# A hand-written order for VectorE and ScalarE in a fused time-mix and feed-forward kernel

## The chip, the cores and the metric

The kernel runs on one core of a Trainium2 chip. A core has engines with a queue of instructions each: TensorE (PE, matrix products; PEld are its weight loads), VectorE (DVE), ScalarE (ACT), GpSimd (POOL), and SyncE (SP), whose queue issues nearly all DMA transfers of this kernel. They meet through semaphores. The metric is the time of one execution on the device, in microseconds, smaller being better. The median of three runs of the kernel before is 883.06 us, the lowest 882.07 and the highest 883.17.

## What is computed

The input `x` holds 4 sequences of 1024 tokens with 512 features. Each token is normalised (`xn`), and two branches are added to `x`. The reference, cut to what matters:

```python
xn = _layernorm(x)
# branch 1: time mixing, HIDDEN = 704
xx = concatenate([xn[:, 1:2], xn[:, :-1]], axis=1) - xn
k = (xn + xx * time_mix_k) @ Wk.T
r = (xn + xx * time_mix_r) @ Wr.T
w = exp(-exp(time_decay))
state_t = state_{t-1} * w + relu(k_t)          # a scan over the tokens
out = (state * r) @ Wv.T
att = (out - mean) * rsqrt(var + EPS) * ln_gamma + ln_beta
# branch 2: feed-forward, 2048 hidden features
D = gelu(float16(xn) @ W0.T + bias0).astype(float16)
ffn = (D @ W1.T + bias1).astype(float16)
return x + att + ffn
```

So each token's mixed input is a blend of its own normalised vector and that of the token before it: `xn + (prior - xn) * m`, which is the same as `xn * (1 - m) + prior * m`.

## The kernel before

The 4096 tokens are worked on in 8 blocks of 512 (two blocks to a sequence); `i` is the block in work, `j = i + 1` the next one, prepared while `i` runs. Inside a block a loop over `n` from 0 to 15 walks through the 16 chunks of 128 hidden features of the feed-forward branch. One iteration puts on TensorE, in this order:

- `up` (L738): the product into the bank `pd` for the chunk two iterations ahead, 8 matmuls. ScalarE then makes gelu of it and a cast (`d`).
- `down` (L766): the products of chunk `n` into the four banks `pe`, which add up over the whole block, 8 matmuls.
- a "piece" of the time-mixing branch. In blocks 1 to 7, n=0 to 4 are the `k` pieces and n=7 to 11 the `r` pieces (`three_pass`, L586: 8 matmuls into `pa`, 4 into `pb`); n=5 and 6 are the two half pieces (`half_pass`, L614: 8 matmuls into `ph`); n=12 to 15 are the output pieces, one for each 128 tokens. In blocks 0 and 1 the output pieces use unsplit operands (`po`), and tokens are dealt with in pairs; from block 2 on they are three-pass products (`out_three_pass`, L682: `oa` and `ob`). In the last block two output pieces share n=12 and two share n=13, and the last four chunks of `down` are left to the end.

The banks `pd`, `pa`, `pb`, `ph`, `oa`, `ob` and `po` come from one pool of four; `pe` from another pool of four.

A piece returns a function, its "follower", that is called one iteration later, behind the next `up`. It empties the banks: `a` on ScalarE (L604), `y` from `pb` and `a` on VectorE (L605); then, for a `k` piece, relu on ScalarE (L607) and the scan on VectorE (L491) into a state tile; for an `r` piece the product with the state (L508) and the split of the result; for an output piece the layer norm's statistics (L303, L304), the reciprocal root on POOL (L297, L298) and three operations on VectorE that end in adding to the residual (L672, L677, L678).

Operands are split into exact parts so that fewer passes of the matrix engine give full precision: `split_x` (L281) makes a truncated value `u` (VectorE, L235), its copy `h` (ScalarE, L284), the rest `l` (VectorE, L285) and a combined term `m` (VectorE, L286).

Besides pieces there is background work, put at chosen iterations: the split of the mixed `r` input (`split_xr`), the next block's load of `x`, its statistics, its normalisation, its 16 transposes (L329), its float16 copies (`x16`), and at the end of a block its mixing (`mixed`, L344, one of four pieces of 128 features at a time). The mixing takes `xx` as the difference of the prior token and the token (L354) and blends twice (L357), all on VectorE, then splits the `k` input. At the head of iteration 14 four ScalarE copies (`ffn_input`) make the next block's `xf`. In block 1 there is more: the `wr` weights are split (`split_kr`) and stored to memory, `wv` is split (`split_wv`), and the low parts of W0 are stored (`store_w0l`). After n=15 four operations on VectorE (`rounded`, L723) take the four sums out of `pe`; in the next block's n=0 and 1, `finish` (L728) adds them to the residual and SP stores the result.

What sets the order: inside `tc.manual_schedule(engines=...)` the named engines issue what the block holds in the order in which it is written; an engine that is not named is ordered by the framework's scheduler. Block 0 and what comes before it name TensorE, VectorE, ScalarE and SyncE. From block 1 on only TensorE and SyncE are named (L831), so VectorE and ScalarE are ordered by the scheduler; POOL is always ordered by it. The end of the kernel (L965) names TensorE and VectorE.

Tiles come from pools with a fixed number of places: 63 `part` tiles (tag `q`) hold the split operands, the states and the weights that stay; 5 `temp` tiles (tag `s`) hold short-lived values; `x` has one place for both the next block's input and the residual. Whoever writes a new tile waits until a place is free.

Of the kernel before, what the change touches and what calls it, by code (L numbers as in the profile page):

```python
# [22 lines left out]
def time_mix_and_gelu_ffn(  # L23
# [30 lines left out]
    nc = tc.nc  # L54
# [226 lines left out]
    def split_x(raw, name):  # L281
        u = truncated(raw, f"u{name}")
        h, l, m = (part(f"{p}{name}") for p in "hlm")
        nc.scalar.copy(h, u)  # L284
        nc.vector.tensor_sub(l, raw, u)  # L285
        nc.vector.scalar_tensor_tensor(m, l.bitcast(F32), -S, u, ALU.mult, ALU.add)  # L286
        return h, l, m
# [55 lines left out]

    def mixed(i, c):  # L344
        t0 = blocks[i][1]
        now = xnT[:, c, 1:]
        if t0 > 0:
            nc.gpsimd.tensor_copy(xnT[:, c, 0:1], last[:, c, :])
        else:
            nc.vector.tensor_copy(xnT[:, c, 0:1], now[:, 0:2][:, 1:2])  # L350
        if t0 + TB < T:
            nc.gpsimd.tensor_copy(last[:, c, :], xnT[:, c, TB : TB + 1])
        xx = temp(f"xx_{i}_{c}")
        nc.vector.tensor_sub(xx, xnT[:, c, :TB], now)  # L354
        xk = temp(f"xk_{i}_{c}")
        for dst, m in ((xk, mk_sb), (now, mr_sb)):
            nc.vector.scalar_tensor_tensor(  # L357
                dst, xx, m[:, c : c + 1], now, ALU.mult, ALU.add
            )
        xks[i, c] = split_x(xk, f"k_{i}_{c}")  # L360
        xrs[i, c] = now

    def split_xr(i, c):
        xrs[i, c] = split_x(xrs[i, c], f"r_{i}_{c}")

# [119 lines left out]


    gs, ghs, ks = {}, {}, {}

# [17 lines left out]
    def gated(j, h, r):  # L506
        g = gs[j, h]
        nc.vector.tensor_mul(g, g, r)  # L508
        if j >= RAW_OUT:
            gs[j, h] = split_x(g, f"g_{j}_{h}")  # L510

    def gated_half(j, st, r):
        if j >= RAW_OUT:
            g = temp(f"gh_{j}")
            nc.vector.tensor_mul(g[:HF], st[:HF], r)
            u, l = temp(f"gu_{j}"), temp(f"gl_{j}")
            nc.vector.tensor_scalar(
                u[:HF].bitcast(I32), g[:HF].bitcast(I32), MASK, None, ALU.bitwise_and
            )
            ghs[j] = part(f"gh_{j}")  # L520
            nc.scalar.copy(ghs[j][:HF], u[:HF])
            nc.vector.tensor_sub(l[:HF], g[:HF], u[:HF])
            nc.scalar.copy(ghs[j][HF:], l[:HF])
            return

        def tokens(ap, odd):
            return ap.rearrange("p (s two t) -> p s two t", two=2, t=P)[:, :, odd, :]

        ghs[j] = part(f"gh_{j}", F32)[:, : NS // 2 * P]
        ghs[j] = ghs[j].rearrange("p (s t) -> p s t", t=P)  # L530
        for odd in range(2):
            nc.vector.tensor_mul(
                ghs[j][odd * HF : (odd + 1) * HF], tokens(st[:HF], odd), tokens(r, odd)
            )

    def raw_k(j, h, pk=None):
        if pk is None:
            pk = bank(f"pk_{j}_{h}")
            for c in range(NC):
                product(pk, raw_w[0, h], xks[j, c], c)  # L540

        def after():
            rk = temp(f"rk_{j}_{h}")
            nc.scalar.activation(rk, pk, AF.Relu)
            scanned(j, h, P, state_tile(j, h), rk)

        return after

    def raw_r(j, h):
        pr = bank(f"pr_{j}_{h}")  # L550
        for c in range(NC):
            state["pr"] = product(pr, raw_w[1, h], xrs[j, c], c)

        def after():
            gated(j, h, pr)

        return after

    def raw_halves(j, sums):
# [15 lines left out]
        def after():  # L575
            both = temp(f"kr_{j}")
            nc.scalar.copy(both, sums[0])
            nc.vector.tensor_add(both, both, sums[1])
            rk, st = temp(f"rk_{j}_{NF}"), temp(f"st_{j}_{NF}")
            nc.scalar.activation(rk[:HF], both[:HF], AF.Relu)  # L580
            scanned(j, NF, HF, st, rk)
            gated_half(j, st, both[HF:])

        return after

    def three_pass(j, kind, h):  # L586
# [15 lines left out]
        def after():  # L602
            a, y = temp(f"a_{j}_{kind}_{h}"), temp(f"y_{j}_{kind}_{h}")
            nc.scalar.activation(a, pa, AF.Copy, scale=1.0 + 1.0 / S)  # L604
            nc.vector.scalar_tensor_tensor(y, pb, -1.0 / S, a, ALU.mult, ALU.add)  # L605
            if kind == 0:
                nc.scalar.activation(y, y, AF.Relu)  # L607
                scanned(j, h, P, state_tile(j, h), y)
            else:
                gated(j, h, y)  # L610

        return after

    def half_pass(j, kind):  # L614
# [13 lines left out]
        def after():  # L628
            a, y = temp(f"a_{j}_{kind}_{NF}"), temp(f"y_{j}_{kind}_{NF}")
            nc.scalar.copy(a[:HF], pa[HF:])  # L630
            nc.vector.tensor_add(y[:HF], pa[:HF], a[:HF])  # L631
            if kind == 0:
                nc.scalar.activation(y[:HF], y[:HF], AF.Relu)
                ks[j] = temp(f"st_{j}_{NF}")
                scanned(j, NF, HF, ks[j], y)
            else:
                gated_half(j, ks.pop(j), y[:HF])

# [27 lines left out]
    def residual(i, s, po):  # L666
# [8 lines left out]

        def rest():
            nc.vector.scalar_tensor_tensor(y, y, rstd, beta_sb, ALU.mult, ALU.add)  # L677
            nc.vector.tensor_add(z, z, y)  # L678

        return rest  # L680

    def out_three_pass(i, s):  # L682
# [16 lines left out]
        def after():  # L699
            a, y = temp(f"oa_{i}_{s}"), temp(f"oy_{i}_{s}")  # L700
            nc.scalar.activation(a, pa, AF.Copy, scale=1.0 + 1.0 / S)
            nc.vector.scalar_tensor_tensor(y, pb, -1.0 / S, a, ALU.mult, ALU.add)
            residual(i, s, y)()

        return after

    def out_piece(i, s):
# [3 lines left out]
        if s % 2 == 0:  # L711
            return lambda: None
        pair = (s - 1, s)
        out_halves(i, pair)

        def after():
            rests = [residual(i, s, pos.pop(s)) for s in pair]
            for rest in rests:
                rest()

# [91 lines left out]
    with tc.manual_schedule(engines=engines):  # L812
        for h in range(FIRST):
            raw_k(0, h, pks[h])()
        first_x16s()
        xf = ffn_input(0)
        raw_r(0, 0)()
        several(split_w0, (0, 0), (0, 1))
        raw_r(0, 1)()
        several(split_w0, (0, 2), (0, 3))  # L820
        w1s = [load_w1(0, n) for n in range(AHEAD)]
        raw_r(0, 2)()
        several(split_w0, (1, 0), (1, 1))
# [5 lines left out]
    for i in range(len(blocks)):  # L829
        with tc.manual_schedule(  # L830
            engines=engines if i == 0 else {nc.tensor.engine, nc.sync.engine}  # L831
        ):
# [25 lines left out]

            def fresh_mixed(c):
                mixed(j, c)  # L860

# [28 lines left out]
            else:  # L890
                order = [(0, h) for h in range(NF)] + [(1, h) for h in range(NF)]
                for k, (kind, h) in enumerate(order):
                    pieces[k + 2 * kind, 0] = [three_pass, i, kind, h]
                    if k > 1:
                        put(k - 2 + 2 * (k > 6), fetch_kr, i, kind, h)
                pieces[5, 0] = [half_pass, i, 0]
                pieces[6, 0] = [half_pass, i, 1]
                put(2, split_xr, i, 0)
                put(4, split_xr, i, 1)
                put(5, split_xr, i, 2)  # L900
                put(5, split_xr, i, 3)
                if j <= LAST:
                    put(2, fetch_x)
                    put(4, stats, *range(NS))
                    put(5, lambda: norm_apply(j, state["x"]))
                    put(6, turn, 0, 2)
                    put(7, turn, 2, 6)
                    put(8, turn, 6, 10)
                    put(9, turn, 10, 14)
                    put(10, turn, 14, 16)  # L910
                mix_at = (11, 12, 13, 14) if i < RAW_OUT else (12, 13, 14, 15)
            if i == 1:
                for g in range(NN // G):
                    put(2 * g, store_w0l, g)
                for h, n in enumerate((3, 6, 8, 9, 10, 11)):
                    put(n, split_wv, h)
            put(11 if j <= LAST else 2, fetch_residual)
            if j <= LAST:
                put(10, x16, j)
                for c, n in enumerate(mix_at):  # L920
                    put(n, fresh_mixed, c)
                put(13, fetch_kr, j, 0, 0)
# [3 lines left out]
            for n in range(NN):  # L926
                ahead = n + AHEAD
                if ahead == NN and j <= LAST:
                    xf = ffn_input(j)
                nxt = (i, ahead) if ahead < NN else (j, ahead - NN)  # L930
                gelu = up(*nxt) if nxt[0] <= LAST else None
                for follow in followers:
                    follow()
                followers = []
# [9 lines left out]
                if two_on[0] <= LAST:  # L944
                    load_w0l(*two_on)
                for s in (2 * n, 2 * n + 1):
                    if s < len(e16s):
                        finish(i - 1, s, e16s[s])
                for s in range(NS):
# [3 lines left out]
                if i == 0 and ahead + 1 < NN:  # L953
                    load_w1_raw(ahead + 1)
                for fn in bg[n]:
                    fn()
                if i == 0:
# [4 lines left out]

    for follow in followers:
        follow()
    with tc.manual_schedule(engines={nc.tensor.engine, nc.vector.engine}):  # L965
# [55 lines left out]
```

## Time and profile before

| What | Value |
|---|---|
| median of the runs | 883.06 us |
| the profiled execution: its time | 882.6 us |
| its span, first to last instruction | 880.8 us |
| granted TensorE clock | 0.997 |
| TensorE busy | 864.6 us, 3760 matmuls |
| VectorE busy | 671.5 us, 1126 instructions |
| ScalarE busy | 389.1 us, 677 instructions |
| GpSimd busy | 73.7 us, 142 instructions |
| DMA | 195.01 MB, 221 GB/s |

The page gives busy time of each engine over the span. A busy TensorE is one with matmuls in flight: a matmul of 512 columns is listed with 389 ns, but in an undisturbed stretch the next one starts 0.227 us after it. For single instructions the timeline gives start, duration, engine, line, operation, output and inputs, and in brackets the idle time before it and what ended it. The table of stretches gives for each stretch its length and the busy time and count of instructions of PE, PEld, DVE, ACT and POOL, then the granted clock, the share of the DMA engines and GB/s. Groups of instructions carry their count, their busy time, the mean in ns of one, and the idle time of the engine just before them.

### The profile page before, as it was taken

The page shows a single profiled execution, that of the slowest core. Times are in us where ns is not written, and L with a number is a line of the kernel's source. Part 1 is how long each engine was busy: PE and PEld are TensorE (multiplying, and loading weights), DVE is VectorE, ACT ScalarE, POOL GpSimd, SP SyncE. Part 2 cuts the span into 40 slices and gives each one's busy share as a digit, 9 for nine tenths or more (in the row PEclk, how much of TensorE's full clock was granted, in tenths as well). Part 3 has the DMA queues.
Part 4 walks back from the last instruction along what each step waited for, and adds up shares of the span by engine and source line. Part 5 has one row for each costly group of instructions (what it writes and reads, how often), then busy time and mean ns, then how long its engine had stood idle before and what let it go on. Part 6 is the DMA issues. An engine that isn't in the chain of part 4 may idle for free.

```text
span 880.8 us, 11076 instructions
## 1 busy us (share of the span) xinstructions
PE 864.6 (98%) x3760; PEld 685.5 (78%) x3760; DVE 671.5 (76%) x1126; ACT 389.1 (44%) x677; POOL 73.7 (8%) x142
## 2 busy tenths in 40 slices
PE   8999999999999999999999999999999999999996
PEld 8676658877578788887888788887888878888885
DVE  5668886899657969598795977859698696975457
ACT  4855533546333543444434454344543444434331
POOL 1100000001111001000110101100011100100001
PEclk9999999999999999999999999999999999999999
DMA  8579657965567555876559665695556966577641
GB/s 264 206 235 336 238 167 259 314 201 170 180 227 269 202 198 179 281 245 222 180 174 341 206 204 191 200 327 179 207 199 205 325 210 196 179 243 280 227 143 49
DMA packets 100164, 195.01 MB, mean 221 GB/s; under 512 B 10991, under 2 KB 25356, under 8 KB 100108
## 3 DMA queue, kind: packets, MB, share of 16 engines
q1 hardware_dynamic: 100048, 194.29, 65.8%
q8 instruction: 30, 0.49, 0.2%
q14 instruction: 26, 0.21, 0.1%
q10 hardware_dynamic: 60, 0.02, 0.0%
HBM read 165.43 MB, written 28.84 MB: 221 GB/s over the span
## 4 chain that ended last, share of the span: by engine, by line
PE 55%; DVE 20%; DMA 3%; issue 2%; POOL 1%; ACT 0%; SPq 0%; DVEq 0%
PE pd L746 15%; PE pe L768 14%; PE pa L592 9%; DVE xnT L329 7%; PE oa L687 6%; PE pb L373 4%; PE ob L695 3%; DMA x<-in_L_attn_x 3%; PE po L646 2%; DVE g L491 1%; DVE y L605 1%; DVE stx L303 1%; PE ob L697 1%; DVE lr L285 1%; DVE y L631 1%
## 5 line engine op out<-in xcount | busy, mean ns | idle before, releaser
L768 PE MATMUL pe<-w,d 128*128 128x512 f32 x1008 | 248.9, 389 | 0.0
L768 PEld LDWEIGHTS pe<-w,d 128*128 128x128 f32 x1008 | 189.1, 188 | 39.6 <-DVE w L170 0.2
L746 PE MATMUL pd<-xf,w0h 128*128 128x512 f32 x512 | 205.2, 401 | 6.0 <-DVE y L631 3.8
L746 PE MATMUL pd<-xf,w0l 128*128 128x512 f32 x512 | 199.5, 390 | 0.0
L756 ACT ACTIVATE d<-pd,late_sb 128x512 f16<-128x512 f32 x128 | 87.7, 685 | 129.0 <-PE pd L746 128.6
L746 PEld LDWEIGHTS pd<-xf,w0h 128*128 128x128 f32 x512 | 96.1, 188 | 37.5 <-DVE y L631 6.4
L605 DVE SCALAR_TENSOR_TENSOR y<-pb,a 128x512 f32<-128x512 f32 x70 | 48.2, 688 | 96.0 <-PE pb L373 88.1
L746 PEld LDWEIGHTS pd<-xf,w0l 128*128 128x128 f32 x512 | 96.2, 188 | 21.4 <-issue 1.9
L604 ACT ACTIVATE a<-pa 128x512 f32<-128x512 f32 x70 | 41.8, 597 | 92.5 <-PE pa L592 92.3
L761 ACT CAST d<-d 128x512 fp32r<-128x512 f16 x128 | 79.3, 620 | 2.6
L329 DVE STREAM_TRANSPOSE xnT<-x 32x512 f32<-32x512 f32 x112 | 78.7, 702 | 2.2
L592 PE MATMUL pa<-hk,kr 128*128 128x512 f32 x140 | 54.5, 389 | 0.0
L592 PE MATMUL pa<-lk,kr 128*128 128x512 f32 x140 | 54.5, 389 | 0.0
L607 ACT ACTIVATE y<-y 128x512 f32<-128x512 f32 x35 | 22.1, 633 | 63.1 <-DVE y L605 63.1
L592 PE MATMUL pa<-lr,kr 128*128 128x512 f32 x120 | 46.7, 389 | 0.0
L592 PE MATMUL pa<-hr,kr 128*128 128x512 f32 x120 | 46.7, 389 | 0.0
L687 PE MATMUL oa<-wv,hg 128*128 128x512 f32 x120 | 46.7, 389 | 0.0
L687 PE MATMUL oa<-wv,lg 128*128 128x512 f32 x120 | 46.7, 389 | 0.0
L297 POOL TENSOR_SCALAR ry<-mvy 128x1 f32<-128x1 f32 x32 | 17.0, 530 | 348.8 <-DVE mvy L304 348.8
L284 ACT CAST hk<-uk 128x512 fp32r<-128x512 f32 x28 | 17.4, 622 | 48.3 <-DVE uk L235 48.3
L373 PE MATMUL pb<-mk,kr 128*128 128x512 f32 x140 | 37.4, 389 | 0.0
L646 PE MATMUL po<-wvraw,g 128*128 128x512 f32 x80 | 35.6, 592 | 0.0
(165 smaller groups left out, 1319.2 us busy)
## 6 DMA issues: line engine op xcount, KB each, us to landing
w<-w1d SPq DMA_DIRECT2D x110, 512.0 KB, 3.7
kr<-krd SPq DMA_DIRECT2D x195, 256.0 KB, 4.9
w0l<-w0d SPq DMA_DIRECT2D x96, 256.0 KB, 4.1
x<-in_L_attn_x SPq DMA_DIRECT2D x32, 256.0 KB, 5.5
w1d<-w SPq DMA_DIRECT2D x16, 512.0 KB, 2.9
xres<-in_L_attn_x SPq DMA_DIRECT2D x32, 256.0 KB, 5.3
krd<-wt SPq DMA_DIRECT2D x30, 256.0 KB, 2.7
out<-xres SPq DMA_DIRECT2D x28, 256.0 KB, 5.4
```

The source lines that it names most:

```text
L329: nc.vector.transpose(dst[i * Q : (i + 1) * Q, :, :, j, :], src[j * Q : (j + 1) * Q, :, :, i, :],)
L373: return nc.tensor.matmul(dst, w[:, c, :], src, start=(c == 0), stop=(c == NC - 1))
L592: nc.tensor.matmul(pa, w[p][:, c, :], xs[j, c][p], start=(c == 0 and p == 0), stop=(c == NC - 1 and p == 1),)
L604: nc.scalar.activation(a, pa, AF.Copy, scale=1.0 + 1.0 / S)
L605: nc.vector.scalar_tensor_tensor(y, pb, -1.0 / S, a, ALU.mult, ALU.add)
L646: nc.tensor.matmul(pos[s], gs[i, h][:, s * P : (s + 1) * P], wv_raw[h], start=(h == 0), stop=False,)
L687: nc.tensor.matmul(pa, gs[i, h][p][:, cols], wv[h][p], start=(h == 0 and p == 0), stop=(h == NF - 1 and p == 1),)
L695: nc.tensor.matmul(pb, gs[i, h][2][:, cols], wv[h][2], start=(h == 0), stop=False)
L746: nc.tensor.matmul(pd, w, xf[c], start=(c == 0 and p == 0), stop=(c == NC - 1 and p == 1),)
L756: nc.scalar.activation(d16, pd, AF.Gelu, bias=b0_sb[:, n : n + 1])
L761: nc.scalar.copy(d, d16)
L768: nc.tensor.matmul(pe[s] if sum_ is None else sum_, d[:, s * P : (s + 1) * P], w1[p][:, cols], start=(n == first and p == 0), stop=(n == e ...
```

## The change

Every block now names all four engines, so that VectorE and ScalarE follow the written order from block 1 to the end. To write a finer order, the followers and the longer jobs become generators: each `yield` marks the end of a step. The loop runs the first step of each follower ahead of gelu, and later, behind the piece's matmuls, `woven` runs one step of each follower and one step of the background jobs in turn until the followers are done; then the rest of the jobs run. In block 0, in iteration 12 of every block, and in iterations 13 to 15 of block 1, followers are run in one go (`finished`) ahead of gelu.

The mixing is computed in its other form. ScalarE scales the token by `1 - m` (`rest_sb`, made at the start of the kernel already) into two temporaries, one for `k` and one for `r`, and VectorE adds the prior token times `m`; the difference `xx` is gone. The mixed `r` input now lies where the prior token lay (`prior`, columns 0 to 511 of the tile) and no longer where the token itself lay.

Background work moves: `split_xr` to n = 2, 2, 3, 3 (in block 1: 2, 3, 5, 5); the statistics become four jobs; the transposes become 16 jobs, in n=6 to 10 three, four, four, three and two (in block 1: none, five, five, five, one); the mixing goes to n = 12 to 15 (in block 1: 12, 13, 15, 15); in block 1 the five `split_kr` go to n = 4, 6, 8, 9, 10 and the six `split_wv` to n = 1, 10, 11, 12, 13, 13, and the normalisation to n=6. The `xf` copies go from the head of n=14 into n=13's mixing, behind its two scalings. The `finish` jobs are taken up with the background jobs, behind the piece.

```diff
@@ split_x
         nc.scalar.copy(h, u)
+        yield
         nc.vector.tensor_sub(l, raw, u)
+        yield
         nc.vector.scalar_tensor_tensor(m, l.bitcast(F32), -S, u, ALU.mult, ALU.add)
@@ mixed
-        xx = temp(f"xx_{i}_{c}")
-        nc.vector.tensor_sub(xx, xnT[:, c, :TB], now)
-        xk = temp(f"xk_{i}_{c}")
-        for dst, m in ((xk, mk_sb), (now, mr_sb)):
-            nc.vector.scalar_tensor_tensor(
-                dst, xx, m[:, c : c + 1], now, ALU.mult, ALU.add
-            )
-        xks[i, c] = split_x(xk, f"k_{i}_{c}")
-        xrs[i, c] = now
+        prior = xnT[:, c, :TB]
+        srcs = []
+        for kind in range(2):
+            j = kind * NC + c
+            srcs.append(temp(f"x{'kr'[kind]}_{i}_{c}"))
+            nc.scalar.activation(srcs[kind], now, AF.Identity, scale=rest_sb[:, j : j + 1])
+        xk, xr = srcs
+        meanwhile()
+        nc.vector.scalar_tensor_tensor(
+            xk, prior, mk_sb[:, c : c + 1], xk, ALU.mult, ALU.add
+        )
+        yield
+        nc.vector.scalar_tensor_tensor(
+            prior, prior, mr_sb[:, c : c + 1], xr, ALU.mult, ALU.add
+        )
+        xks[i, c] = yield from split_x(xk, f"k_{i}_{c}")
+        xrs[i, c] = prior
@@ new helpers
+    def finished(*steps):
+        for work in steps:
+            for _ in work or ():
+                pass
+
+    def woven(works, jobs):
+        def steps():
+            for job in jobs:
+                yield from job() or ()
+                yield
+
+        others = steps()
+        while works:
+            works = [w for w in works if next(w, works) is None]
+            next(others, None)
+        finished(others)
@@ three_pass, its follower
                 nc.scalar.activation(y, y, AF.Relu)
+                yield
                 scanned(j, h, P, state_tile(j, h), y)
             else:
-                gated(j, h, y)
+                yield from gated(j, h, y)
@@ residual
-        def rest():
-            nc.vector.scalar_tensor_tensor(y, y, rstd, beta_sb, ALU.mult, ALU.add)
-            nc.vector.tensor_add(z, z, y)
-
-        return rest
+        yield
+        nc.vector.scalar_tensor_tensor(y, y, rstd, beta_sb, ALU.mult, ALU.add)
+        nc.vector.tensor_add(z, z, y)
@@ out_three_pass, its follower
             nc.vector.scalar_tensor_tensor(y, pb, -1.0 / S, a, ALU.mult, ALU.add)
-            residual(i, s, y)()
+            yield
+            yield from residual(i, s, y)
@@ the blocks
         with tc.manual_schedule(
-            engines=engines if i == 0 else {nc.tensor.engine, nc.sync.engine}
+            engines=engines
         ):
...
-            def fresh_mixed(c):
-                mixed(j, c)
+            def fresh_mixed(c, n):
+                if i > 0 and n == NN - AHEAD - 1:
+                    return mixed(j, c, next_xf)
+                return mixed(j, c)
...
-                        put(k - 2 + 2 * (k > 6), fetch_kr, i, kind, h)
+                        early = (4, 6, 8, 9, 10)[h] if i == kind == 1 else k - 2 + 2 * (k > 6)
+                        put(early, fetch_kr, i, kind, h)
...
-                put(2, split_xr, i, 0)
-                put(4, split_xr, i, 1)
-                put(5, split_xr, i, 2)
-                put(5, split_xr, i, 3)
+                for c, n in enumerate((2, 3, 5, 5) if i == 1 else (2, 2, 3, 3)):
+                    put(n, split_xr, i, c)
...
-                    put(4, stats, *range(NS))
-                    put(5, lambda: norm_apply(j, state["x"]))
-                    put(6, turn, 0, 2)
-                    put(7, turn, 2, 6)
-                    put(8, turn, 6, 10)
-                    put(9, turn, 10, 14)
-                    put(10, turn, 14, 16)
-                mix_at = (11, 12, 13, 14) if i < RAW_OUT else (12, 13, 14, 15)
+                    for s in range(NS):
+                        put(4, stats, s)
+                    put(6 if i == 1 else 5, lambda: norm_apply(j, state["x"]))
+                    turns = (0, 5, 5, 5, 1) if i == 1 else (3, 4, 4, 3, 2)
+                    for k in range(sum(turns)):
+                        unit = next(n for n in range(5) if k < sum(turns[: n + 1]))
+                        put(6 + unit, turn, k, k + 1)
+                mix_at = (12, 13, 15, 15) if i == 1 else (12, 13, 14, 15)
...
-                for h, n in enumerate((3, 6, 8, 9, 10, 11)):
+                for h, n in enumerate((1, 10, 11, 12, 13, 13)):
                     put(n, split_wv, h)
@@ the loop over n
-                for follow in followers:
-                    follow()
+                works = [follow() for follow in followers]
+                if i == 0 or n == NN - NS or (n > NN - NS and i < RAW_OUT):
+                    finished(*works)
+                    works = []
+                else:
+                    works = [w for w in works if next(w, works) is None]
...
-                for s in (2 * n, 2 * n + 1):
-                    if s < len(e16s):
-                        finish(i - 1, s, e16s[s])
+                jobs = [
+                    lambda s=s: finish(i - 1, s, e16s[s])
+                    for s in (2 * n, 2 * n + 1)
+                    if s < len(e16s)
+                ]
...
-                for fn in bg[n]:
-                    fn()
+                woven(works, jobs + bg[n])
```

## The prediction

> **What bounds the kernel now.** I read the page first, then the waits, then the stretches in which TensorE loses time, then single rows.
>
> ```profile
> span 880.8 us, 11076 instructions
> PE 864.6 (98%) x3760; PEld 685.5 (78%) x3760; DVE 671.5 (76%) x1126; ACT 389.1 (44%) x677; POOL 73.7 (8%) x142
> PE pd L746 <- DVE y L631: 3.8, 5, 1.5
> PE pd L746 <- DVE y L605: 2.0, 6, 0.4
> ```
>
> TensorE is the bound: 864.6 of 880.8 us. The two waits name what interrupts it: the next `pd` needs a PSUM bank that `y` on VectorE has not yet emptied. To price this I took the stretches by iteration starts (columns: us, then busy us and count of PE, PEld, DVE, ACT, POOL):
>
> ```profile
> 175.35:209.20 33.85, 33.02 (x142) 25.89 (x140) 31.62 (x55) 19.86 (x36) 1.55 (x4) 1.00 0.58 186
> 286.08:307.57 21.49, 19.67 (x85) 15.62 (x84) 19.65 (x30) 11.47 (x20) 0.18 (x1) 1.00 0.59 197
> 392.80:412.81 20.01, 19.67 (x86) 15.61 (x85) 18.40 (x32) 11.03 (x20) 0.54 (x4) 1.00 0.63 209
> 498.03:518.62 20.59, 19.66 (x86) 15.61 (x84) 18.77 (x29) 11.46 (x20) 0.18 (x1) 1.00 0.61 205
> 603.85:625.01 21.16, 19.63 (x85) 15.61 (x84) 19.52 (x33) 11.51 (x20) 0.54 (x4) 1.00 0.58 202
> 710.24:730.50 20.26, 19.66 (x85) 15.61 (x84) 18.48 (x28) 11.21 (x20) 0.18 (x1) 1.00 0.61 211
> 294.09 0.50 PE L746 MATMUL pd<-xf,w0h 128*128 128x512 f32 x1 [1.51 <-DVE y L631]
> ```
>
> The last five stretches are n=7 to 9 of blocks 2 to 6. Undisturbed, such an iteration takes 6.346 us (28 matmuls 0.2267 apart; 307.57 to 313.92), three take 19.04, so the losses are 2.45, 0.97, 1.55, 2.12 and 1.22: 8.31 us. Block 1 (n=7 to 11) takes 33.85 against 31.73: 2.12. VectorE is over 90% busy there: the 16 transposes stand in front of `y`. Together 10.4 us is all that a better order can gain before the tail.
>
> **The change, part by part.** Instructions on VectorE start 0.60 us apart when independent (868.12, 868.72 below), 0.72 when one needs the last; a transpose takes 0.715, a truncation 0.45.
>
> *Mixing.*
>
> ```profile
> L354 DVE TENSOR_TENSOR xx<-xnT 128x512 f32<-128x512 f32 x24 | 16.4, 682 | 0.0
> L357 DVE SCALAR_TENSOR_TENSOR xk<-xx,mix_sb,xnT 128x512 f32<-128x512 f32 x24 | 17.7, 738 | 0.0
> L425 ACT ACTIVATE ar<-pt,rest_sb 128x512 f32<-128x512 f32 x4 | 2.4, 718 | 0.0
> ```
>
> Seven blocks of four pieces lose 28 x 0.682 = 19.1 us of VectorE and put 56 x 0.718 = 40.2 us on ScalarE, which is 44% busy; the fused operations stay at 0.74. Neither is a gain by itself: it counts only where TensorE waits. The first block runs Identity between other functions with no table load in between, so I count none.
>
> [...]
>
> *Order, blocks 2 to 6.* I added up VectorE's written list per iteration. n=8: `y` starts 0.28 after the iteration (as at 425.50, 425.77), then 0.72 for `y`, 0.72 product, 0.45 truncation, 0.72, 0.72, and four transposes 2.86: 6.5 of 6.35. n=2 and 3 come to 6.4 and 6.9, n=4 to 6.3, n=5 to 4.8 of 5.44, n=6 to 5.8, n=7 to 6.5, n=9 to 5.9. Each list begins with `y`, which TensorE needs only an iteration later, so lateness of up to some 5 us is free and at most 0.6 arises. The 8.31 go. The `x` load keeps its place on SP; its arrival at n=4 (480.66 against 480.81) is behind `y` and the scan.
>
> *What is late next: the end of a block.* Before, the four `e` (sums out of the `pe` banks) slipped in early; now they follow all of n=15's mixing. ScalarE's order puts the scaling behind gelu and its cast:
>
> ```profile
> 447.94 0.39 PE L746 MATMUL pd<-xf,w0h 128*128 128x512 f32 x1
> 450.01 0.69 ACT L756 ACTIVATE d<-pd,late_sb 128x512 f16<-128x512 f32 x1 [2.86 <-PE pd L746]
> 450.73 0.62 ACT L761 CAST d<-d 128x512 fp32r<-128x512 f16 x1
> 457.23 1.98 PE L768 MATMUL pe<-w,d 128*128 128x512 f32 x8
> ```
>
> From 447.94: cast at 2.79, scaling 3.31 to 4.03 (cast and next operation start 0.52 apart). VectorE finishes the residual's first half at 3.4, waits, runs `xk` from 4.06, residual (0.66, 0.78), `xr` 6.10, truncation 6.76, 7.21, 7.93, then the `e` from 8.53, ending 9.20, 9.80, 10.40, 11.00. TensorE wants the banks at 9.29 (457.23) and every 0.45 after it: the last comes 0.35 to 0.45 late, and each restart cost 0.11 before (first spacing 0.34 for 0.23 after 294.09). Bounds 0 to 1.0 a block; I take 0.55, five times: 2.75. While waiting, the residuals are the only other work, so no cover is left. SP: the `out` stores of n=0 wait for VectorE until some 2.4 us into n=1, with the `kr` loads for n=2 behind them, 3 us later than at 461.07; they land in 4.9 and are needed 10 us into n=1. POOL's column copy runs a block ahead (428.38, right after the last reading of that column) and now follows `xr`'s splits at n=3, early enough. The four `xf` copies, moved behind n=13's scalings, end at 4.5 + 4 x 0.52 = 6.6; the next block's `pd` reads the first at 7.48: nothing, covered by n=13's own matmuls.
>
> *Block 1.* The pool of 63 parts is what the new places meet. After n=3 it holds 16 `w0h`, 12 `w0l`, 5 raw `wr`, 6 `wvraw`, 12 `k` splits, 3 `wv`, 3 states, 6 `r` splits: 63. The scan of n=4 needs a 64th, and the next to come free is an `m` part when `pb` starts at 5.44: VectorE stands from 1.7 to 5.9 us, with `y`'s successors behind it. Going on by hand: n=5 starts its `y` 5.8 late, relu then delays gelu on ScalarE, n=6 and n=7 run 6.6 and 7.1 late in their `y`, and `pd` of n=8 waits 1.5 us; n=10's `x16` copies stand before n=11's `a`, and `pb` waits 1.4. At n=9 and n=10 the margin is only 0.7 to 1.0. The `kr` splits come one or two iterations later, and SP stands in their stores until at most 2.6 us into the next iteration, in front of its `w` load, which waits for `pe` until 3.6 anyway: nothing, and the next three-pass piece gets its terms 1.5 us or more before it starts. So 2.9 in place of 2.12; at the block's end, by the same steps, 0.65. Bounds: 0 (were a part free) to 6 (margin missed twice). The row nearest is block 1's own 2.12; I take 2.9.
>
> *Block 0.* Its VectorE queue was ordered already. The scaling delays `xf` by some 0.7 us against a margin of as much: 0.1.
>
> *The tail.*
>
> ```profile
> 862.93 0.69 DVE L702 SCALAR_TENSOR_TENSOR oy<-ob,oa 128x512 f32<-128x512 f32 x1 [0.28 <-PE ob L697]
> 866.91 0.69 DVE L678 TENSOR_TENSOR xres<-xres,oy 128x512 f32<-128x512 f32 x1
> 867.52 0.68 DVE L702 SCALAR_TENSOR_TENSOR oy<-ob,oa 128x512 f32<-128x512 f32 x1
> 868.12 0.68 DVE L970 TENSOR_TENSOR base<-pe,b_sb 128x512 f32<-128x512 f32 x1
> 868.72 0.68 DVE L303 BATCH_NORM_STATS2 sty<-oy 128x6 f32<-128x512 f32 x1
> 877.13 0.42 DVE L731 TENSOR_TENSOR xres<-xres,e 128x256 f32<-128x256 f32 x1
> ```
>
> Here VectorE sets the end: busy without a gap from 866.91 to 877.55. Before, piece 2's residual ran while TensorE made piece 3. Now both pieces take their first step together: `y` of 3 (possible at 866.85) stands in front of the statistics of 2. Four instructions (0.60, 0.10, 0.66, 0.66 at the filled spacing) move behind 866.85: 2.0 us; if nothing fills the dependent gaps (0.12 each on some eight), 3.0. The rows show filling (`base` between `y` and its statistics), so I take 2.2, bounds 1.2 and 3.2.
>
> Sum: -8.31 + 2.75 - 2.12 + 2.9 + 0.65 + 0.1 + 2.2 = -1.8 us against the profiled execution's 882.6: 880.8. That execution is 0.46 below the median 883.06, which gives 881.3 from the median. I forecast 881.0.
>
> **The rivals.**
> *A part comes free* (chance 0.2): my count of 63 is one too high, block 1 loses nothing but its end. Sum -1.8 - 2.9 = -4.7: 878. For it: the trace of before shows no wait on a part. Against: the count closes exactly.
> *The block's end costs more, slower* (0.23): one more ScalarE operation (0.52) or a late `ry` from POOL ahead of the scaling or the residual delays the `e` of five blocks at once. Each 0.1 us costs 0.5. At 0.76 us more a block it is 884.8, slower than the bound; I price it at 1.0 more: 886. For it: the chain ScalarE, VectorE, POOL crosses engines four times in 7.5 us, and `ry` takes 1.9 us (435.88 to 437.75). Against: ScalarE's six operations there (0.60, 0.69, 0.62, 0.62 and two scalings) fill 4.0 of 7.48 us.
> *Block 1's margin is missed* (0.19): VectorE 1 us later by n=9 makes `pd` wait at two more starts and at `pb`: 3 more, 884.
> *My forecast* (0.38).
>
> **How the numbers follow.** A run of this kernel tells about 0.2% (1.8 us) from no change: below 881.3 is faster, above 884.8 slower. Forecast 0.38 (its own range 879 to 883: 0.21 faster, 0.16 same, 0.01 slower); free part 0.2 (0.19 faster, 0.01 same); block's end 0.23 (0.03 same, 0.20 slower); block 1 0.19 (0.02 faster, 0.09 same, 0.08 slower). Faster 0.42, same 0.29, slower 0.29. The range 877.5 to 887 takes all four centres and leaves 0.1 on either side.
>
> **What the profile after would show.** Right: no `pd` waiting for `y` at n=7 to 9 of blocks 2 to 6; VectorE idle before `xk` with a ScalarE scaling as releaser, some 0.7 us, in n=13 to 15; small waits of `pe` for `e` at n=0; a scan in n=4 of block 1 waiting about 4 us for TensorE's `pb`; and in the tail VectorE idle before the last residual's `y`, the stores 2 us later behind TensorE's end. Wrong: a table load among the scalings, transposes still in front of `y`, or the `e` ending well after 11.0.

## The result and the profile after

The kernel with the change takes 887.98 us, the median of 8 runs (885.95 to 889.37). The kernel before, run beside it, takes 883.12 us (8 runs, 882.07 to 884.29). The ratio is 1.0052, with a 95% interval of 1.0038 to 1.0066: the change costs 4.9 us. The forecast of 881.0 us had the sign wrong, and 887.98 lies 1 us above its range.

The page of the kernel after, first line and busy times:

```profile
span 887.2 us, 11092 instructions
PE 868.7 (98%) x3760; PEld 686.6 (77%) x3760; DVE 671.3 (76%) x1098; ACT 431.5 (49%) x733; POOL 75.2 (8%) x142
```

The span is 6.4 us longer. VectorE has 28 instructions fewer and is as busy as before; ScalarE has 42.4 us more. TensorE is still the bound, so the question is again what interrupts it. The waits of TensorE from block 0 on that bear on the change:

```profile
PE pb L383 <- ACT a L638: 2.1, 1, 2.1
PE pe L806 <- DVE e L763: 1.7, 5, 0.3
PE pe L806 <- ACT d L794: 1.1, 1, 1.1
PE ph L655 <- ACT hr L284: 0.7, 1, 0.7
PE pd L784 <- ACT xf L379: 0.3, 1, 0.3
```

The waits of `pd` for `y`, 5.8 us before, are gone. In their place stand waits of `pe` for the sums `e`, five times (the ends of blocks 2 to 6), and two single ones in block 1, of `pb` and `ph`. The wait of 1.1 us is the end of block 1: the list puts it down to `d`, but that matmul starts (252.29) 0.10 us after the first `e` is done (251.51 and 0.68), and the wait is gone when the sums stand earlier, as shown below. The wait of `pd` for `xf` is in block 0. That the gain arrived is seen in the stretches n=7 to 9 of blocks 2 to 6 (columns as in the table of before):

```profile
292.45:311.49 19.04, 19.04 (x85) 15.77 (x84) 17.17 (x27) 7.88 (x13) 0.00 (x0) 1.00 0.68 211
398.79:417.83 19.04, 19.04 (x86) 15.77 (x85) 16.83 (x26) 8.42 (x14) 0.00 (x0) 1.00 0.66 219
505.12:524.16 19.04, 19.04 (x86) 15.77 (x85) 17.13 (x26) 7.90 (x13) 0.00 (x0) 1.00 0.67 228
611.45:630.49 19.04, 19.04 (x85) 15.77 (x84) 17.10 (x27) 7.90 (x13) 0.00 (x0) 1.00 0.69 222
717.78:736.82 19.04, 19.04 (x86) 15.77 (x85) 17.14 (x26) 7.89 (x13) 0.00 (x0) 1.00 0.71 234
```

Each takes 19.04 us, with TensorE busy throughout: all of the 8.31 us came. So 14.7 us of span went elsewhere. The table cuts both traces at the first `pd` product of an iteration; the last column is what the prediction's terms say for the same stretch.

| Stretch, us | before | after | difference | predicted |
|---|---|---|---|---|
| start, to the first `pd` | 33.17 | 34.51 | +1.3 | 0 |
| block 0 | 99.43 | 100.56 | +1.1 | +0.1 |
| block 1, n=0 to 15 | 110.73 | 114.05 | +3.3 | +0.8 |
| n=0 of block 2 (end of block 1) | 6.48 | 8.22 | +1.7 | +0.65 |
| n=1 of block 2 to n=0 of block 7 | 529.65 | 526.71 | -2.9 | -5.6 |
| block 7, n=1 to 12 | 77.52 | 77.52 | 0 | 0 |
| tail, from the last `pd` on | 23.82 | 25.65 | +1.8 | +2.2 |

In the fifth row the five n=0 iterations of blocks 3 to 7 take 7.40 to 7.45 us where they took 6.35: 1.07 more each in the mean, not the forecast 0.55.

**The end of a block.** Before, the scheduler put the sums between other work. In the n=15 that starts at 447.94 the first began 2.83 us after the iteration, the second 6.93 and the last two together from 8.13 on:

```profile
450.77 0.66 DVE L725 TENSOR_TENSOR e<-pe,b_sb 128x512 f16<-128x512 f32 x1
454.87 0.68 DVE L725 TENSOR_TENSOR e<-pe,b_sb 128x512 f16<-128x512 f32 x1
```

After the change: VectorE from the last mixing of block 2 on, and the `down` of block 3 that waits:

```profile
351.86 0.75 DVE L363 SCALAR_TENSOR_TENSOR xk<-xnT,mix_sb,xk 128x512 f32<-128x512 f32 x1 [0.55 <-ACT xk L360]
355.03 0.69 DVE L286 TENSOR_TENSOR lk<-xk,uk 128x512 fp32r<-128x512 f32 x1
355.64 0.68 DVE L736 SCALAR_TENSOR_TENSOR oy<-ob,oa 128x512 f32<-128x512 f32 x1
356.24 0.68 DVE L288 SCALAR_TENSOR_TENSOR mk<-lk,uk 128x512 fp32r<-128x512 f32 x1
356.84 2.47 DVE L763 TENSOR_TENSOR e<-pe,b_sb 128x512 f16<-128x512 f32 x4
357.58 2.52 PE L806 MATMUL pe<-w,d 128*128 128x512 f32 x8 [0.34 <-DVE e L763]
```

`xk` starts 4.08 us after its iteration (347.78), held up by the scaling on ScalarE: forecast 4.06. But between `lk` and `mk` stands `oy`, the sum of the last output piece, which is written in n=0 of block 3. Each block has a hand-written order of its own; the orders of two blocks are not tied to each other, so the scheduler let this one step of the next block in. The four sums start 9.06 us after the iteration and not 8.53.

**Block 1.** VectorE's `y` and scan in n=4; then ScalarE's queue and TensorE at n=10 and 11, and the stretch behind it (third figure from the right: the granted clock):

```profile
160.87 0.69 DVE L639 SCALAR_TENSOR_TENSOR y<-pb,a 128x512 f32<-128x512 f32 x1 [1.90 <-PE pb L383]
166.53 1.28 DVE L519 TENSOR_TENSOR_SCAN g<-late_sb,carry,y 128x512 f32<-128x512 f32 x1 [4.97 <-PE pb L383]
209.68 2.16 ACT L344 CAST x<-xnT 128x512 f16<-128x512 f32 x4
211.75 0.58 ACT L638 ACTIVATE a<-pa 128x512 f32<-128x512 f32 x1
212.38 1.80 PE L383 MATMUL pb<-mr,wt 128*128 128x512 f32 x4 [2.06 <-ACT a L638]
214.00:218.00 4.00, 4.00 (x15) 3.21 (x14) 3.41 (x7) 2.63 (x5) 0.00 (x0) 0.73 0.14 54
```

The scan stood 4.97 us for the 64th part, as counted. In n=11, seven iterations later, VectorE is still late, the four `x16` copies run in front of `a`, and `pb` waits 2.06 us for its bank. From 212.72 to 216.13 the granted clock is 0.50. That costs another 1.6 us: n=11 and 12 take 17.8 us together, and 16.2 in the kernel with the tail one by one (below), whose `pb` waits 2.0 us there without such a window (granted clock 1.00 from 205 to 218).

**The tail.** VectorE in the last pieces:

```profile
868.44 0.68 DVE L736 SCALAR_TENSOR_TENSOR oy<-ob,oa 128x512 f32<-128x512 f32 x1
871.37 0.69 DVE L736 SCALAR_TENSOR_TENSOR oy<-ob,oa 128x512 f32<-128x512 f32 x1 [2.25 <-PE ob L731]
883.63 0.42 DVE L769 TENSOR_TENSOR xres<-xres,e 128x256 f32<-128x256 f32 x1
```

`oy` of piece 2 is done at 869.1, its statistics stand behind `oy` of piece 3, and VectorE is idle for 2.25 us.

### The profile page after: what moved, and what is told of

Read it like the earlier page. It is cut to its first block, busy times and chain, and to the rows that moved or that the text cites. A ratio compares the mean times of both kernels' runs of the same rounds, so it can differ in the third digit from the quotient of the medians.

```text
span 887.2 us, 11092 instructions
## 1 busy us (share of the span) xinstructions
PE 868.7 (98%) x3760; PEld 686.6 (77%) x3760; DVE 671.3 (76%) x1098; ACT 431.5 (49%) x733; POOL 75.2 (8%) x142
## 4 chain that ended last, share of the span: by engine, by line
PE 80%; DVE 10%; ACT 4%; DMA 2%; issue 2%; SPq 0%; ACTq 0%; DVEq 0%
PE pd L784 22%; PE pe L806 21%; PE pa L626 13%; PE pb L383 7%; PE oa L721 5%; PE po L682 3%; PE ph L655 2%; PE ob L729 2%; PE pk L383 2%; DVE xnT L331 2%; PE pr L383 1%; PE ob L731 1%; ACT d L794 1%; DMA wvraw<-in_L_attn_Wv 1%; DVE e L763 1%
## 5 line engine op out<-in xcount | busy, mean ns | idle before, releaser
L806 PE MATMUL pe<-w,d 128*128 128x512 f32 x1008 | 252.5, 392 | 3.3 <-DVE e L763 1.7
L806 PEld LDWEIGHTS pe<-w,d 128*128 128x128 f32 x1008 | 187.2, 188 | 49.5 <-DVE e L763 9.2
L299 POOL TENSOR_SCALAR ry<-mvy 128x1 f32<-128x1 f32 x32 | 20.2, 630 | 436.2 <-DVE mvy L306 436.2
L363 DVE SCALAR_TENSOR_TENSOR xk<-xnT,mix_sb,xk 128x512 f32<-128x512 f32 x28 | 21.1, 752 | 34.1 <-ACT xk L360 34.0
L519 DVE TENSOR_TENSOR_SCAN g<-late_sb,carry,y 128x512 f32<-128x512 f32 x20 | 25.7, 1284 | 18.3 <-ACT y L641 13.3
```

What stands on the lines that cost most here:

```text
L519: nc.vector.tensor_tensor_scan(dst[:hw], w_sb[:hw, h : h + 1].to_broadcast([hw, TB]), src[:hw], 0.0 if t0 == 0 else carry[:hw, h : h + 1], ...
L806: nc.tensor.matmul(pe[s] if sum_ is None else sum_, d[:, s * P : (s + 1) * P], w1[p][:, cols], start=(n == first and p == 0), stop=(n == e ...
```

## The experiments

Kernel before in these runs: 883.14 us (31 runs) beside the first four, 883.12 (12 runs) beside the kernel with the copies later, 883.42 (23 runs) beside the other four. Ratios are to it. Lengths of blocks and iterations are from the one profiled execution of each kernel.

**One half of the change at a time.** The first kernel is the one before with the new `mixed` alone, VectorE and ScalarE ordered by the scheduler; the second is the kernel after with the old `mixed`:

```diff
-            nc.scalar.activation(srcs[kind], now, AF.Identity, scale=rest_sb[:, j : j + 1])
+        nc.vector.tensor_sub(xx, xnT[:, c, :TB], now)
...
+            xk, xx, mk_sb[:, c : c + 1], now, ALU.mult, ALU.add
```

> The kernel before, with the mixing alone changed (scaling on ScalarE, result in the prior token's place); order of VectorE and ScalarE from block 1 on by the scheduler as before. Theory A (the written order puts work that TensorE needs behind waits; the mixing itself is harmless): 883 us, within 2 of before, with the waits of pd for y at n=7 to 9 of blocks 2 to 6 unchanged (8.3 us lost there). Theory B (the mixing's scaling on ScalarE is what costs): 887 or more, and most of the 5 us that the change cost show here already.

> The changed kernel with the old mixing (difference xx and both blends on VectorE), all else in the written order. Theory A: the part that is missing in n=4 of block 1 and the tail stay; the sums at the block's end come some 0.7 us earlier because nothing waits for the scaling, so about 883 to 884, 4 below the changed kernel. Theory B: the order's gain stands free, 880 or less.

The mixing alone: 884.70 us (883.07 to 885.95), ratio 1.0017 [1.0008, 1.0027]. The order alone: 881.81 us (879.75 to 882.82), ratio 0.9982 [0.9973, 0.9992]. Waits of TensorE, the first two of the one and the first of the other:

```profile
PE pd L752 <- DVE y L637: 3.9, 6, 1.4
PE pd L752 <- DVE y L611: 2.0, 6, 0.4
PE pb L379 <- ACT a L634: 1.9, 1, 1.9
```

With the mixing alone TensorE waits for `y` as before, although VectorE's busy time fell from 671.5 to 654.3 us. The order alone removes these waits, and its n=0 iterations of blocks 2 to 7 sum to 39.6 us against 45.3 with both halves. So the halves cost +1.6 and -1.3 us alone and +4.9 together. The first number fits theory A (within 2 us of before, waits unchanged); of its 1.6 us only 0.3 is traced to a wait that is new (of `pd` for `xf`, in block 0); the rest stays open. The second lies between its two theories. At the end of block 2 the sums start 8.02 us after the iteration with the old mixing and 9.06 with the new. About 0.55 of that is VectorE's wait for the scaling. Another 0.48 is the step `oy`, which stands behind the sums in the kernel with the order alone although its blocks are ordered one by one there too. This only matters because the written order keeps the sums behind the mixing.

**A part that comes free.** In block 1 the first `wv` is split at n=14 and not at n=1, so that the scan of n=4 finds a part:

```diff
-                for h, n in enumerate((1, 10, 11, 12, 13, 13)):
+                for h, n in enumerate((14, 10, 11, 12, 13, 13)):
```

> The changed kernel with the first split of wv moved from n=1 to n=14 of block 1, so that 60 parts and not 63 are held after n=3. Theory A: the scan of n=4 no longer waits 5 us for TensorE's pb, VectorE is 5 us earlier through block 1, the wait of ph at n=6 (0.9), of pb at n=11 (2.1) and the slow matmuls after it (1.2) go: 884, some 4 below the changed kernel. Theory B (and any theory by which block 1 loses to VectorE's sheer load): no change, 888.

883.44 us (881.71 to 884.18), ratio 0.9999 [0.9986, 1.0011]: 4.5 us faster than with the change. VectorE's scan in n=4:

```profile
160.25 1.29 DVE L519 TENSOR_TENSOR_SCAN g<-late_sb,carry,y 128x512 f32<-128x512 f32 x1 [0.70 <-ACT y L641]
```

This fits theory A. The idle time before the scan is 0.70 us in place of 4.97. Block 1 takes 108.86 us, n=6 to 11 are undisturbed, and the waits of `ph` and `pb` are off the list. The edit also takes a split's work out of n=1, but that work is not the cause: in the kernel after, VectorE was idle for 1.90 us ahead of `y` in n=4 (the line at 160.87), so it had caught up before it met the missing part. Both waits were consequences of that part.

**The sums ahead of the mixing.** At every block's end the four `rounded` become the first jobs of n=15:

```diff
+                if n == NN - 1 and not tail:
+                    e16s = []
+                    jobs = [lambda s=s: e16s.append(rounded(i, s, pe[s])) for s in range(NS)]
...
-            if not tail:
-                e16s = [rounded(i, s, pe[s]) for s in range(NS)]
```

> The changed kernel with the four sums taken out of pe ahead of the mixing of n=15 and no longer behind it, in every block. Theory A: each of the five ends of blocks 2 to 6 gives back 1.05 us and that of block 1 about 1.5: 881, 7 below the changed kernel. Theory B: VectorE waits for the scaling as before and loses the same, 887 to 888.

881.00 us (878.14 to 881.8), ratio 0.9972 [0.996, 0.9983], as theory A has it. All n=0 iterations take 6.35 or 6.48 us, the end of block 1 included, and block 1 itself is unchanged at 114.07. So 7.0 us lay in the sums' place.

**Only the slip between two blocks.** One hand-written order over all blocks instead of one for each. This moves `oy` behind the four sums and, on ScalarE, the copy `hk` ahead of `oa`, at every block's end; in VectorE's end of block 1 it moves two statistics behind the sums:

```diff
-    for i in range(len(blocks)):
-        with tc.manual_schedule(
-            engines=engines
-        ):
+    with tc.manual_schedule(engines=engines):
+        for i in range(len(blocks)):
```

> The changed kernel with its hand-written order in one piece over all blocks and not one piece for each block, so that nothing of the next block comes between a block's last steps: VectorE then makes the four sums before the output piece's sum of the next block's n=0 (one swap per block end), and ScalarE the copy of xk's high part before that piece's scaling. Theory A (the excess of a block's end over the forecast, 7.41 against 6.9 us, is that output sum, which slipped in ahead): first iterations of blocks 3 to 7 at 6.8 to 6.95, that of block 2 at 7.5 to 8.2, time 885 (884 to 886). Rival B (the sums wait for the mixing alone and the slip hides beside a wait): first iterations stay at 7.3 to 7.4, time 887.5 to 888.5.

883.87 us (882.67 to 885.84), ratio 1.0006 [0.9996, 1.0016]. VectorE at the end of block 2:

```profile
354.30 0.69 DVE L288 SCALAR_TENSOR_TENSOR mk<-lk,uk 128x512 fp32r<-128x512 f32 x1
354.91 2.48 DVE L763 TENSOR_TENSOR e<-pe,b_sb 128x512 f16<-128x512 f32 x4
357.30 0.68 DVE L736 SCALAR_TENSOR_TENSOR oy<-ob,oa 128x512 f32<-128x512 f32 x1
```

The iteration n=15 starts at 346.32 here, so the sums start 8.59 us after it; the prediction had 8.53. The n=0 iterations of blocks 3 to 7 take 6.95 us, 0.60 over the undisturbed length (forecast 0.55). Theory A holds for the place; the time is 0.1 us below its range. The slip alone is 0.48 in each of five blocks and 0.47 at the end of block 1, 2.8 us. The rest of the time's gain fits block 1 (112.53, no half-speed window in this execution: the granted clock was 1.00 from 205 to 218).

**The tail one by one.** From n=13 of the last block each follower runs to its end before the next:

```diff
-                if i == 0 or n == NN - NS or (n > NN - NS and i < RAW_OUT):
+                if i == 0 or n == NN - NS or (n > NN - NS and (i < RAW_OUT or i == LAST)):
```

> The changed kernel with one edit: from n=13 of the last block on, the follow-ups of a piece run to their end one after another, not a step at a time. Theory A (in turn, the last output pieces' normalisations each wait for the next, and the last of them frees VectorE late): the stretch from n=15's last up-projection to the end goes from 25.7 us back to about 23.8, and the time to 886 (885 to 887). Rival B (the tail is longer because VectorE comes to it late, whatever the order in it): no change, 888.

884.48 us (883.95 to 887.22), ratio 1.002 [1.001, 1.003]. VectorE, with the last statistics of piece 2 running while TensorE makes piece 3:

```profile
864.66 0.69 DVE L736 SCALAR_TENSOR_TENSOR oy<-ob,oa 128x512 f32<-128x512 f32 x1 [0.27 <-PE ob L731]
865.39 0.69 DVE L305 BATCH_NORM_STATS2 sty<-oy 128x6 f32<-128x512 f32 x1
869.26 0.68 DVE L736 SCALAR_TENSOR_TENSOR oy<-ob,oa 128x512 f32<-128x512 f32 x1
```

The tail is 23.75 us, as before the change: A is right on the place and on 1.9 us. The time fell by 3.5, more than A's range allows; block 1, which the edit doesn't touch, took 112.51 us in this profile, without the half-speed window (granted clock 1.00 from 205 to 218). Executions with a mean granted clock of 0.991 to 0.993 were three of twelve here (887.0 to 887.2 us) and four of eight in the kernel with the change. Without them the medians are 884.4 and 886.5 us, 2.1 apart, so some 1.4 of the 3.5 us is the share of such executions.

**The copies later.** In block 1 the `x16` copies stand at n=11, behind that unit's split, with the part still missing:

```diff
-                put(10, x16, j)
+                put(11 if i == 1 else 10, x16, j)
```

> The changed kernel with one edit: in block 1 the four fp16 copies of the next block's x stand at n=11, behind that unit's split of Wv, and not at n=10, so that the pair's scaled sum of n=11 no longer stands behind them on ScalarE. The output weight's 64th part stays at n=1. Theory A (the second loss of block 1 is this queue on ScalarE, 2.06 us, and the half-speed window that follows it in some executions is a consequence): n=11 at 6.35 to 6.6 us and n=12 at 7.5, the wait of n=6 for the 64th-wide product (0.7 us) unchanged, no half-speed window behind n=11, time 885 (884 to 886) and a narrower spread. Rival B (VectorE itself is late by the 3.4 us that the part takes at n=1 and the copies only stand in between): the wait at n=11 turns into one for VectorE's y or its transposes of like size, 887 to 888.

886.68 us (885.8 to 887.37), ratio 1.0038 [1.0025, 1.0052]: neither theory's number. n=11 takes 6.53 us (9.27 in the kernel after), no clock window follows (the next `pd` products start 0.23 us apart, from 209.66 to 211.25), and the spread is narrower, all as A has it. But a new wait stands first in TensorE's list, and n=13 takes 11.06 us where it took 9.48:

```profile
PE pd L784 <- ACT xf L379: 1.5, 1, 1.5
```

The queue at n=11 was the place at which the lateness was paid, not its cause. Moved past it, the 2.1 us of copies delay `a` of n=12 and then the `xf` copies of n=13. Block 1 takes 112.22 us, hardly less than the 112.51 of a kernel that keeps the queue and has no window. B is right in kind, with another place. Of the two edits only the part that comes free ends it.

**All three edits, and the same with the old mixing.** The part at n=14, the sums ahead, the tail one by one; then these three with `mixed` as before the change.

> The changed kernel with three edits at once: the 64th part of Wv's first weight split at n=14 and not at n=1 of block 1, the four sums of the down-projection ahead of the last mixing at every block's end, the tail's follow-ups one by one. Theory A (three separate waits in the written order, one place each): the gains add, 888.0 - 4.5 - 7.0 - 1.8 = 874.7 (873 to 876.5), block 1 at 108 to 109 us, first iterations of blocks 2 to 7 at 6.35 to 6.5, tail at 23.8. Rival B (one shortage of VectorE time that moves to the next place when one is mended): 878 or more, with new waits in block 1 or the tail.

> The three edits of the kernel with all three, but with the mixing of before (difference and two blends on VectorE, nothing scaled on ScalarE). From the runs so far: 881.8 for the order alone, less 1.8 for the tail, 3 to 3.5 for block 1 and about 1 for the blocks' ends = 875.5 (874 to 877). Theory A (once the sums stand ahead of it, it makes no difference which engine scales): within 1 us of the kernel with all three. Rival B (VectorE still lacks the 0.6 us per mixing that ScalarE takes off it): 878 or more, with first iterations of blocks above 6.5 us. Rival C (the wait for the scaling costs wherever it stands): 873 or less.

With the new mixing 873.63 us (872.89 to 873.94), ratio 0.9886 [0.9872, 0.99]; with the old one 873.30 us (873.08 to 874.17), ratio 0.9885 [0.9871, 0.9899]. The page of the first, the busy line of the second, and VectorE of the first at the end of block 2:

```profile
span 871.1 us, 11105 instructions
PE 860.8 (99%) x3760; PEld 686.7 (79%) x3760; DVE 672.9 (77%) x1098; ACT 431.7 (50%) x733; POOL 74.6 (9%) x142
```

```profile
PE 860.8 (99%) x3760; PEld 686.7 (79%) x3760; DVE 691.3 (79%) x1126; ACT 396.8 (46%) x677; POOL 75.0 (9%) x142
```

```profile
342.36 0.68 DVE L763 TENSOR_TENSOR e<-pe,b_sb 128x512 f16<-128x512 f32 x1
344.61 1.88 DVE L763 TENSOR_TENSOR e<-pe,b_sb 128x512 f16<-128x512 f32 x3
346.40 0.74 DVE L363 SCALAR_TENSOR_TENSOR xk<-xnT,mix_sb,xk 128x512 f32<-128x512 f32 x1
```

The gains add to within 1.1 us of the expected 874.7. All n=0 iterations take 6.35 or 6.48, block 1 108.65, the tail 23.74. This is 9.8 us faster than the kernel before. The two mixings lie within each other's spread: theory A of the second holds, although 873.30 is below the 874 to 877 that its sum gave. The order is what gains; the scaling on ScalarE gives nothing, although it does take 18.4 us off VectorE (691.3 - 672.9).

## Why the prediction was wrong

**Right.** The 8.31 us in blocks 2 to 6 went to the last hundredth. The count of 63 parts was right: the scan waited 4.97 us (forecast 4.2). The chain at a block's end held to `lk` within 0.1 us. The tail came to 1.8 (forecast 2.2), by the mechanism described. The mixing as such was priced at no gain, and with the waits gone it has none; its 19.1 us of VectorE measured 18.4. No table load stands among the scalings: both traces have three, the last at 33.0 and 34.3 us.

**Wrong: the block's end.** The step that failed is "truncation 6.76, 7.21, 7.93, then the `e` from 8.53". It read the written order of a block as if nothing else could come between. The next block's first VectorE step could, and did: 0.48 in each of five blocks by the run with one order over all blocks. With 0.05 more that the chain itself cost, 0.55 became 1.07: 2.6 us in all. This was the place of the rival "the block's end costs more", at half of its price; the causes that it named, one more ScalarE operation or a late `ry`, were not what delayed the sums. At the end of block 1 the term 0.65 measured 1.74; 0.47 of that was the slip (7.75 without it). The other 0.6 was mis-sized: its two mixing pieces run one behind the other in n=15 and the sums start, even without the slip, 11.4 us after the iteration, 1.9 us into the next.

**Wrong: block 1.** "So 2.9 in place of 2.12": the 2.12 went but for 0.25 (108.86 us with a part free, 110.73 before), but the missing part cost 5.2 (114.05 less 108.86) and not 2.9. Without the half-speed window it costs 3.7 (112.51 less 108.86, the first from the kernel with the tail one by one). Single terms: `pd` of n=8 waiting 1.5 measured nothing; `pb` of n=11 at 1.4 measured 2.06; `ph` of n=6 waiting 0.7 (its split of `xr` stands behind the late scan) was not in the sum; and the granted clock of 0.5 behind the `pb` wait, 1.6 us, was not thought of. Of the kernel after, the four executions with a mean granted clock of 0.991 took 888.3 to 889.4 us, the four at 0.995 to 0.997 took 885.95 to 887.63. Only the profiled one shows where the clock was 0.50: from 7.92 to 14.75, here, and from 881.73 to the end. That the other three had it here too is not shown.

**Wrong, partly by chance.** Start and block 0 add 2.5 us to the profiled execution. The start has the same TensorE code as before; it measured 32.99 to 34.62 in the eleven profiles. In the start the granted clock was 0.50 for 6.83 us in the profile after (7.92 to 14.75) and for 3.41 us in the one before (8.34 to 11.75). So most of this is spread between executions: the profiled one took 889.37, 1.4 us above the median. Block 0 took 99.8 to 100.6 us with the new mixing and 99.4 to 100.1 with the old one. The scaling's share that the traces show is 0.3 us (forecast 0.1): `pd` waits for `xf` once in block 0 in each kernel with the new mixing, for 0.2 to 0.3 us, and in none with the old one.

The profiled span missed the sum by 8.2 us: 3.7 at the ends of blocks, 2.5 in block 1, 2.4 in start and block 0, less 0.4 in the tail. That the first three point the same way is partly luck.

## What to carry to other kernels

An order written by hand must put first what the bounding engine waits for: here four sums of 0.6 us each stood behind a chain that crosses engines, and moving them gained 7 us. Look at where hand-written stretches meet: between two of them the scheduler may still slip something in. Count the fixed places of tiles against the written order: one part too few cost 3.7 to 5.2 us. Moving 18.4 us of work off an engine that was not the bound was worth nothing here, and the handover that it brought had to be placed.

## What the runs showed of the hardware

In the profile of the kernel after, the granted clock was 0.50 from 7.92 to 14.75, from 212.72 to 216.13 and from 881.73 to the end, and 1.00 in the rest. The second of these stretches, 3.41 us long, followed a wait of 2.06 us in the midst of a busy kernel; `pd` products in it start 0.43 us apart and not 0.227:

```profile
213.98 0.63 PE L784 MATMUL pd<-xf,w0h 128*128 128x512 f32 x1
214.41 0.63 PE L784 MATMUL pd<-xf,w0l 128*128 128x512 f32 x1
```

Five profiles have the wait of `pb` in n=11. Behind 2.06 us (the kernel after) and 1.80 (the sums ahead) came a stretch at a lower clock: the means from 214 to 218 are 0.73 and 0.77. Behind 2.0 (the tail one by one) and 1.8 (one order over all blocks) the clock was 1.00 from 205 to 218. Behind 1.9 (the order alone) there was none either, by an estimate from its page: a mean of 0.997 over 879.1 us lacks about 2.6 us of full clock, of which the last of the page's 40 slices, below 0.9, takes at least 2.2; 3.41 us at half would be 1.7. So the length of the wait does not explain it alone. What decides is not shown.

The written order makes the same 1126 VectorE instructions busy for 691.3 us where the scheduler's order took 671.5. Operations that need the last one's result start 0.72 us apart (`sty` and `mvy` of the kernel after, 349.61 and 350.33), independent ones 0.60 (`oy` and `mk` there, 355.64 and 356.24), at a duration of 0.68 or 0.69. The single durations add up to 722.1 and 719.2 us, so what differs is how much neighbours overlap: the scheduler mixed chains, and a chain written in a row overlaps less. This cost no time that a run here shows, since TensorE is the bound.

A scaling measures 0.71 us on ScalarE (L360 of the kernel after) and a difference on VectorE 0.68 (L354 of the kernel before), and the kernels with and without it take 873.6 and 873.3 us: no run here shows a loss by the operation itself, only by the wait for it.
